# Layer 2 of a four-layer graph network: scores transposed, one constant shift in the softmax, row sums by a column of ones

## The chip, the cores and the metric

The kernel runs on one core of one Trainium2 chip. The metric is the device time of one execution in microseconds. The kernel before takes 2988.76 us, the median of three runs (2983.72, 2988.76 and 2989.16).

The engines are called by their names in the profile: PE is TensorE (matrix products and transposes; PEld are its weight loads), DVE is VectorE, ACT is ScalarE, POOL is GpSimd, SP is SyncE, whose queue issues most loads and stores.

## The reference, cut to what matters

The input x has 32 graphs of 512 nodes with 256 features, in float32. One adjacency matrix of 512 by 512 integers holds for all graphs; about 1 entry in 16 is set, and the diagonal is. Four layers follow each other, and after each one stands `x = layernorm(x + layer(x))`:

- Layer 0: attention with 8 heads under the mask, then a two-matrix network with two layer norms of its own.
- Layer 1: attention whose scores are sums of two numbers, one for each node, through a leaky ReLU.
- Layer 2, the one that changes: full scores between all nodes.
- Layer 3: like layer 1 with 4 heads, and an ELU at its end.

Layer 2 computes, for each graph:

```python
h1, h2, h3 = x @ W1, x @ W2, x @ W3          # 512 x 256 each
e = leaky_relu(h1 @ h2.T, 0.2)               # 512 x 512
e = where(adj > 0, e, -1e12)
out = relu(softmax(e, axis=-1) @ h3)
```

A softmax doesn't change when the same number is subtracted from every score of a row. Any number that keeps the exponentials in the range of float32 will do; the row's maximum always does.

## The kernel before, in words

**Tiles.** A graph's x lies in SBUF as 4 blocks (`NC`) of 128 nodes on the partitions, with 256 features (`KC` = 2 blocks of 128). `transposed` (L857 to L871) turns it on PE into a buffer with the features on the partitions. A matrix product on PE takes two operands with the contracted index on the partitions: one of 128 columns is loaded as weights, the other, of up to 512 columns, streams through; the result lands in one of 8 PSUM banks of 512 columns. Each float32 product is two records in the profile, so the counts of matmuls are twice those of the calls; transposes are one record each.

**Layer 2** (`layer2`, L1186 to L1243). W1 and W2 are multiplied once, in `prepare`, into `l2m`, with the sign turned (L847, `scale=-1.0`). So the kernel before works on the negative scores:

- L1190: q = x·l2m, transposed; L1191: v = x·W3.
- For each block c of 128 query nodes: L1200 makes their negative scores against all 512 keys in one bank. ACT scales them by 0.2 into `lo` (L1203), DVE takes the minimum of both (L1206), which is the negative leaky ReLU. L1208, one fused DVE operation, adds the mask and brings each row's minimum along in an accumulator. ACT takes the exponential with that minimum as bias, and sums each row in its own accumulator (L1213). DVE inverts the sum (L1216).
- The exponentials have the queries on the partitions, and the last product needs the keys there. So L1223 transposes them, 16 blocks of 128x128, and ACT copies four banks to `pT` (helper line L854, shown as p<-bank).
- L1234 multiplies by v, two query blocks in one bank; ACT takes the ReLU with the inverted sum as scale (L1239), and POOL adds x (`add`, L924).

Layer 1 (L1158 to L1184) already has the other form: its exponentials have the keys on the partitions, v carries a column of ones (L1161, a POOL memset), L1175 multiplies with 257 columns so that column 257 is the row sum, and DVE inverts it out of the bank (L1180).

**The order of the work.** Every instruction is first entered in a plan: engine, a duration in ns, what it reads and writes, and for transfers a lag until they land. The planner (`place`, L507 to L609) simulates the engines with these durations and emits each engine's instructions in one fixed order. Up to `WAYS` = 5 graphs are in flight. A graph may begin when the one 5 places before it has ended in the plan. Among instructions that could start at the same time, the one with the earliest due time goes first; due times come from `PACE`, `TENTHS`, `START` and `LAST` (numbers in us at the head of the file). PE has different tilings (full array, 32-row, 32- or 64-column parts); `STAY` is what the planner holds against changing the tiling.

**Buffers.** `KINDS` (L659 to L665) gives the number of buffers of each kind: 5 for x (`x`), 8 of 128x2048 (`p`), 18 small ones (`rs`), and so on, plus 8 banks. A graph's result is stored out of its x buffer at L1326, with a lag of 3000 ns in the plan.

**Ranges.** The fast path is followed by a check: some layers use forms that only hold in a range, and `fit`, `far` and `odd` collect whether all values were inside. If not, `general_path` runs after it.

Of the kernel before, what the change touches and what calls it, by code (L numbers as in the profile page):

```python
# [9 lines left out]
FP = mybir.dt.float32  # L10
BF = mybir.dt.bfloat16
I32 = mybir.dt.int32
# [10 lines left out]
R_MIN, R_MAX = 1e-30, 1e20  # L23
H0, H3 = 8, 4
# [3 lines left out]
PACE = 90.76  # L28
START = (0, 17.91, 74.63, 79.1, 135.8)
LAST = ()  # L30
STAY = 3.96
TENTHS = (0, 30.43, 93, 94.94, 170.51, 206.64, 280.32, 312.71, 390.11, 382.2, 480.41)
# [411 lines left out]
class Plan:  # L444
# [62 lines left out]
    def place(self, urgency, ways, stay=0.0, run=True):  # L507
# [35 lines left out]
        while todo:  # L543
# [58 lines left out]
            ended[op.graph] = max(ended.get(op.graph, 0.0), done)  # L602
# [9 lines left out]
def fast_path(  # L612
# [47 lines left out]
        "x": (5, [P, NC, C]), "y": (7, [P, NC, C]), "v": (3, [P, NC, C + 2 * H3]),  # L660
# [15 lines left out]
    nc.gpsimd.memset(eps, EPS)  # L676
    ones = const.tile([P, P], FP, name="ones")
# [47 lines left out]
    odd = keep("odd", [P, NC])  # L725

    def prepare():
# [34 lines left out]
        for m in range(NC):  # L762
            bank = Slot("bank")

            def run(bank=bank, m=m):
# [5 lines left out]
                [bank], [(edge_t, m)])  # L771

# [20 lines left out]
        for c in range(NC):  # L793
            off = Slot("e")
            dve(690, lambda c=c: nc.vector.tensor_scalar(
                T(mask)[:, c, :], T(raws[c // 2])[:, c % 2, :].bitcast(I32), 0.0, BIG, ALU.is_le, ALU.mult),
                [(raws[c // 2], c)], [(mask, c)])
# [39 lines left out]
        for k in range(KC):  # L837
            bank = Slot("bank")

            def run(bank=bank, k=k):  # L840
# [6 lines left out]
                T(l2m)[:, k, :], T(bank)[:, :C], AF.Copy, scale=-1.0), [bank], [(l2m, k)])  # L847
        load(l2w3, lambda t: t, rows(l2_w3))
        scored(l3w, l3_w, l3_a, H3)
# [153 lines left out]

    def skip(n):

        for _ in range(n):
            plan(DMA, 0, None)

    def layer0(xs, at_once):
# [58 lines left out]
        def check():  # L1068
            r = T(rinv)[:, :NC * H0]
            nc.vector.scalar_tensor_tensor(fit, r, R_MIN, fit, ALU.is_gt, ALU.min)  # L1070
            nc.vector.scalar_tensor_tensor(fit, r, R_MAX, fit, ALU.is_lt, ALU.min)
        dve(370, check, [rinv], [], True)
# [113 lines left out]
    def layer2(xs):  # L1186
        xT = transposed(xs)
        qT, v, p, pT, y = Slot("t"), Slot("v"), Slot("p"), Slot("p"), Slot("y")
        for k in range(KC):
            project_t(l2m, k * P, xT, qT, k)  # L1190
        project(xT, l2w3, 0, C, v)  # L1191
        rinvs = []
        for c in range(NC):
            bank, lo, es = Slot("bank"), Slot("e"), Slot("e")
            low, tot, rinv = Slot("rs"), Slot("rs"), Slot("rs")
            rinvs.append(rinv)

            def run(bank=bank, c=c):
                for k in range(KC):
                    nc.tensor.matmul(T(bank), T(qT)[:, k, c * P:(c + 1) * P], T(xT)[:, k, :],  # L1200
                                     start=(k == 0), stop=(k == KC - 1))
# [3 lines left out]

            dve(690, lambda bank=bank, lo=lo, es=es: nc.vector.tensor_tensor(  # L1206
                T(es), T(bank), T(lo), ALU.min), [bank, lo], [es])
            dve(780, lambda es=es, low=low, c=c: nc.vector.tensor_tensor_reduce(  # L1208
                T(es), T(es), T(mask)[:, c, :], 1.0, TOP, ALU.add, ALU.min, T(low)[:, 0:1]),
                [es, (mask, c)], [es, low], True)  # L1210

            def exp(es=es, low=low, tot=tot, rinv=rinv, c=c):
                nc.scalar.activation(T(p)[:, c, :], T(es), AF.Exp, bias=T(low)[:, 0:1],  # L1213
                                     scale=-1.0, accum_out=T(tot)[:, 0:1])
            act(935, exp, [es, low], [(p, c), tot])
            dve(160, lambda tot=tot, rinv=rinv: nc.vector.reciprocal(  # L1216
                T(rinv)[:, 0:1], T(tot)[:, 0:1]), [tot], [rinv])
        for m in range(NC):
            bank = Slot("bank")

            def run(bank=bank, m=m):
                for c in range(NC):
                    nc.tensor.transpose(T(bank)[:, c * P:(c + 1) * P],  # L1223
                                        T(p)[:, c, m * P:(m + 1) * P], ident)
# [182 lines left out]
```

## Time and profile before

| | before |
|---|---|
| device time, median of 3 | 2988.76 us |
| span of the profiled execution | 2983.3 us |
| PE busy | 2901.5 us, 97% |
| PE weight loads busy (beside PE) | 1645.9 us, 55% |
| DVE busy | 2371.4 us, 79% |
| ACT busy | 1962.9 us, 66% |
| POOL busy | 946.7 us, 32% |
| mean granted TensorE clock | 0.990 |

A row of the groups reads: line, engine, operation, output<-inputs, shapes, count | busy us, mean ns of one | idle time of the engine just before, and what ended it. Matmuls overlap on PE, so the mean length of one is longer than the time it holds the engine; the distance from one start to the next tells that. In a waits line stand engine and what it was about to do, what it waited for, the sum in us, how often, and the longest. The span is the time from the first to the last instruction on the chip.

### The profile page before, as it was taken

To read this page: it belongs to the slowest core of one execution; us is meant where nothing else is said; L and a number is where in the kernel's file an instruction comes from. 1 tells how busy PE (TensorE), PEld (TensorE's weight loads), DVE (VectorE), ACT (ScalarE), POOL (GpSimd) and SP (SyncE) were. 2 spreads that over 40 slices of the span, in tenths; PEclk is the share of its full clock that TensorE was granted. 3 is DMA by queue.
4 is the path that set the end of the run, shared out by engine and by line. 5 is a ranking of instruction groups with operands and counts; after the bars stand their busy time and mean duration, and the time that the engine had idled before them with its cause. 6 is when DMAs were issued, how large, how long until landed. Compare 5 with 4: busy or idle time off the path is not lost.

```text
span 2983.3 us, 41104 instructions
## 1 busy us (share of the span) xinstructions
PE 2901.5 (97%) x14770; PEld 1645.9 (55%) x14770; DVE 2371.4 (79%) x4138; ACT 1962.9 (66%) x4359; POOL 946.7 (32%) x865
## 2 busy tenths in 40 slices
PE   7899999999999999999999999999999999999895
PEld 3455555555555555555555555555555555555552
DVE  5567788888887888888888888887888888877785
ACT  4656776666776666776666776666776666776562
POOL 0222343322333322333322333322333322333211
PEclk9999999999999999999999999999999999999998
DMA  6545665566565566666566565566665566563232
GB/s 170 115 89 108 145 133 118 128 147 139 126 138 115 128 147 139 130 135 122 127 148 139 127 141 117 127 147 133 131 138 117 127 147 140 128 138 80 52 89 72
DMA packets 93714, 375.75 MB, mean 126 GB/s; under 512 B 8768, under 2 KB 44736, under 8 KB 57664
## 3 DMA queue, kind: packets, MB, share of 16 engines
q0 software_dynamic: 44640, 292.57, 50.0%
q1 hardware_dynamic: 48864, 80.49, 8.0%
q8 instruction: 118, 1.93, 0.3%
q14 instruction: 92, 0.75, 0.1%
HBM read 63.38 MB, written 17.10 MB: 27 GB/s over the span
## 4 chain that ended last, share of the span: by engine, by line
PE 93%; DVE 3%; DMA 2%; ACT 1%; issue 0%; POOL 0%; SPq 0%; ACTq 0%; DVEq 0%
PE bank L893 15%; PE bank L879 11%; PE bank L996 9%; PE bank L1049 8%; PE bank L1175 8%; PE bank L1234 7%; PE bank L1278 7%; PE bank L1200 7%; PE bank L866 5%; PE bank L1102 4%; PE bank L1090 4%; PE bank L1021 2%; PE bank L1223 2%; PE bank L979 2%; PE bank L1253 1%; PE bank L947 1%
## 5 line engine op out<-in xcount | busy, mean ns | idle before, releaser
L934 POOL DMA_DIRECT2D p<-p x310 | 280.7, 908 | 1228.5 <-issue 290.2
L1042 DVE TENSOR_TENSOR p<-p,edge_t 128x2048 f32<-128x2048 f32 x256 | 602.5, 2355 | 78.9 <-ACT p L1000 78.6
L1000 ACT ACTIVATE p<-bank 128x512 f32<-128x512 f32 x1024 | 559.7, 597 | 137.7 <-PE bank L996 137.5
L854 ACT ACTIVATE t<-bank 128x512 f32<-128x512 f32 x640 | 372.4, 594 | 367.2 <-PE bank L879 147.3
L924 POOL TENSOR_TENSOR y<-y,x 128x512 f32<-128x512 f32 x192 | 339.0, 1769 | 377.6 <-ACT y L1239 173.9
L907 DVE BATCH_NORM_STATS2 st<-y 128x6 f32<-128x256 f32 x768 | 315.3, 411 | 67.7 <-POOL y L924 60.1
L1269 DVE TENSOR_TENSOR p<-p,edge_t 128x2048 f32<-128x2048 f32 x128 | 292.9, 2288 | 3.3
L996 PE MATMUL bank<-t,t 32*128 32x512 f32 x2048 | 294.4, 643 | 0.0
L917 ACT ACTIVATE x<-y,rs,rs 128x256 f32<-128x256 f32 x512 | 283.4, 595 | 7.2 <-DVE rs L914 6.5
L1262 DVE TENSOR_SCALAR p<-p,e,e 128x512 f32<-128x512 f32 x512 | 252.0, 545 | 36.6 <-DMA p<-row 32.6
L1049 PE MATMUL bank<-p,v 128*32 128x512 f32 x2048 | 269.3, 607 | 11.8 <-DVE p L1042 11.7
L1175 PE MATMUL bank<-v,p 128*128 128x257 f32 x1024 | 249.5, 389 | 11.8 <-DVE p L1168 11.8
L1278 PE MATMUL bank<-p,v 128*64 128x512 f32 x1024 | 236.5, 603 | 12.6 <-DVE p L1269 12.6
L854 ACT ACTIVATE v<-bank 128x258 f32<-128x258 f32 (+2 forms) x384 | 171.8, 455 | 111.7 <-PE bank L893 108.5
L1200 PE MATMUL bank<-t,t 128*128 128x512 f32 x512 | 238.7, 599 | 0.0
L879 PE MATMUL bank<-t,wqkv 128*128 128x512 f32 x512 | 233.0, 606 | 3.2 <-ACT t L854 3.2
L1175 PEld LDWEIGHTS bank<-v,p 128*128 128x128 f32 x1024 | 190.8, 193 | 73.9 <-issue 29.7
L1234 PE MATMUL bank<-v,p 128*128 128x256 f32 x1024 | 230.2, 382 | 0.0
L1234 PEld LDWEIGHTS bank<-v,p 128*128 128x128 f32 x1024 | 191.6, 190 | 49.1 <-ACT t L854 20.5
L917 ACT ACTIVATE y<-y,rs,rs 128x256 f32<-128x256 f32 x256 | 138.9, 595 | 62.9 <-DVE rs L914 62.9
L996 PEld LDWEIGHTS bank<-t,t 32*128 32x128 f32 x2048 | 81.1, 183 | 166.6 <-issue 76.5
L866 PEld LDWEIGHTS bank<-ident,x 128*128 128x128 f32 x1024 | 117.4, 142 | 99.4 <-issue 61.3
(116 smaller groups left out, 4487.1 us busy)
## 6 DMA issues: line engine op xcount, KB each, us to landing
p<-p POOLq DMA_DIRECT2D x248, 1024.0 KB, 7.6
p<-row SPq DMA_DIRECT2D x32, 1024.0 KB, 8.9
p<-p POOLq DMA_DIRECT2D x62, 512.0 KB, 5.7
x<-in_x_dram SPq DMA_DIRECT2D x32, 512.0 KB, 3.9
out_dram<-x SPq DMA_DIRECT2D x32, 512.0 KB, 2.9
e<-row SPq DMA_DIRECT2D x32, 256.0 KB, 6.7
t<-in_adj_dram SPq DMA_DIRECT2D x4, 256.0 KB, 6.3
wqkv<-in_L_gnn_w_qkv_dram SPq DMA_DIRECT2D x1, 768.0 KB
```

Of the source, the lines that this page charges most:

```text
L854: act(170 + n * 0.84, lambda: nc.scalar.activation(to(T(dst)), frm(T(src)), AF.Copy), [src], writes)
L879: nc.tensor.matmul(T(bank), T(w)[:, i, col:col + P], T(xT)[:, i, :], start=(i == 0), stop=(i == KC - 1))
L893: nc.tensor.matmul(T(bank)[:, j * width:(j + 1) * width], T(xT)[:, k, (c0 + j) * P:(c0 + j + 1) * P], T(w)[:, k, col:col + width], start=( ...
L917: act(600, lambda c=c: nc.scalar.activation(T(dst)[:, c, :], T(y)[:, c, :], AF.Identity, bias=T(nm)[:, c:c + 1], scale=T(rs)[:, c:c + 1]), ...
L996: nc.tensor.matmul(T(banks[j]), T(kT)[r, g, m * P:(m + 1) * P], T(qT)[r, g, :], start=True, stop=True)
L1000: act(600, lambda j=j: nc.scalar.activation(T(p)[:, j, :], T(banks[j]), AF.Exp, scale=1.0 / math.sqrt(D0)), [banks[j]], [(p, j)])
L1042: dve(2420, lambda p=p, m=m: nc.vector.tensor_tensor(T(p), T(p), T(edge_t)[:, m, :].unsqueeze(1).to_broadcast([P, J, N]), ALU.mult), [p, ( ...
L1049: nc.tensor.matmul(T(av)[j * D0:(j + 1) * D0, :], T(v)[:, m, h * D0:(h + 1) * D0], T(p)[:, j, :], start=(m == 0), stop=(m == NC - 1))
L1175: nc.tensor.matmul(T(bank)[:, :C + 1], T(p)[:, m, c * P:(c + 1) * P], T(v)[:, m, 2:C + 3], start=(m == 0), stop=(m == NC - 1))
L1200: nc.tensor.matmul(T(bank), T(qT)[:, k, c * P:(c + 1) * P], T(xT)[:, k, :], start=(k == 0), stop=(k == KC - 1))
L1234: nc.tensor.matmul(T(bank)[:, j * C:(j + 1) * C], T(pT)[:, m, c * P:(c + 1) * P], T(v)[:, m, :C], start=(m == 0), stop=(m == NC - 1))
L1278: nc.tensor.matmul(T(av)[i * D3:(i + 1) * D3, :], T(q)[:, m0 + m, 2 * H3 + h * D3:2 * H3 + (h + 1) * D3], T(p)[:, 2 * m + i, :], start=(m0 ...
```

## The change

The scores of layer 2 are computed with the keys on the partitions (the two operands of the product swap places). Then the exponentials come out in the layout that the last product needs as weights, and the 16 transposes and four copies of each graph go. A maximum along a row can't be taken there, since a row now lies across partitions. So one constant, 72, is subtracted from all scores, and the row sums come from a column of ones beside v, as in layer 1. The constant only works within limits: the inverted row sums are compared with `R2_MIN` and `R2_MAX`, and the columns of W3 with a bound; outside of them the general path runs. The mask is made from the transposed adjacency, with the other sign.

Four further edits concern the plan: a sixth buffer for x, a lag of 8000 ns instead of 3000 for the store, a graph's end in the plan that no longer includes the lag of its last transfer, and new numbers at the head of the file.

```diff
@@ -21,15 +21,18 @@
 TOP = 3e38
 S_MAX = 40.0
 R_MIN, R_MAX = 1e-30, 1e20
+SHIFT = 72.0
+R2_MIN, R2_MAX = 1.25e-37, 1e31
+V_MAX = 41.0
 H0, H3 = 8, 4
 
 
 WAYS = 5
-PACE = 90.76
-START = (0, 17.91, 74.63, 79.1, 135.8)
-LAST = ()
-STAY = 3.96
-TENTHS = (0, 30.43, 93, 94.94, 170.51, 206.64, 280.32, 312.71, 390.11, 382.2, 480.41)
+PACE = 90.30
+START = (0, 22.9, 53.29, 85.04, 134.37)
+LAST = (-0.21, 0.21)
+STAY = 4.86
+TENTHS = (0, 26.21, 86.69, 92.24, 176.51, 212.02, 277.3, 313.49, 381.31, 382.21, 490.27)
 @with_exitstack
 def general_path(
     ctx: ExitStack,
@@ -599,7 +602,7 @@
             left.remove(op.rank)
             while front[op.graph] not in left and left:
                 front[op.graph] += 1
-            ended[op.graph] = max(ended.get(op.graph, 0.0), done)
+            ended[op.graph] = max(ended.get(op.graph, 0.0), t + op.ns + SIGNAL)
             if not left:
                 del todo[op.graph]
                 order.remove(op.graph)
@@ -657,7 +660,7 @@
 
 
     KINDS = {
-        "x": (5, [P, NC, C]), "y": (7, [P, NC, C]), "v": (3, [P, NC, C + 2 * H3]),
+        "x": (6, [P, NC, C]), "y": (7, [P, NC, C]), "v": (3, [P, NC, C + 2 * H3]),
         "t": (9, [P, KC, N]), "p": (8, [P, 4, N]), "e": (4, [P, N]),
         "st": (6, [P, NC, 6]), "mv": (6, [P, NC, 2]), "rs": (18, [P, NC]),
         "e1": (6, [P, NC * H3]), "gs": (2, [P, NC * H3]), "ri": (3, [P, NC * H0]),
@@ -674,6 +677,8 @@
     make_identity(nc, ident)
     eps = const.tile([P, 1], FP, name="eps")
     nc.gpsimd.memset(eps, EPS)
+    shift = const.tile([P, 1], FP, name="shift")
+    nc.gpsimd.memset(shift, -SHIFT)
     ones = const.tile([P, P], FP, name="ones")
     nc.gpsimd.memset(ones, 1.0)
 
@@ -722,7 +727,7 @@
 
 
     edge_t, mask = keep("edge_t", [P, NC, N], BF), keep("mask", [P, NC, N], BF)
-    odd = keep("odd", [P, NC])
+    odd = keep("odd", [P, NC + 1])
 
     def prepare():
         def load(dst, to, src, lag=15000):
@@ -769,6 +774,9 @@
             plan(PE, 440, run, [edges], [bank])
             dve(690, lambda bank=bank, m=m: nc.vector.tensor_copy(T(edge_t)[:, m, :], T(bank)),
                 [bank], [(edge_t, m)])
+            dve(400, lambda m=m: nc.vector.tensor_scalar(
+                T(mask)[:, m, :], T(edge_t)[:, m, :], 1.0, BIG, ALU.subtract, ALU.mult),
+                [(edge_t, m)], [(mask, m)])
 
 
 
@@ -792,9 +800,6 @@
 
         for c in range(NC):
             off = Slot("e")
-            dve(690, lambda c=c: nc.vector.tensor_scalar(
-                T(mask)[:, c, :], T(raws[c // 2])[:, c % 2, :].bitcast(I32), 0.0, BIG, ALU.is_le, ALU.mult),
-                [(raws[c // 2], c)], [(mask, c)])
             dve(690, lambda c=c, off=off: nc.vector.tensor_tensor(
                 T(off), T(edges)[:, c, :], T(raws[c // 2])[:, c % 2, :].bitcast(I32), ALU.not_equal),
                 [edges, (raws[c // 2], c)], [off])
@@ -844,8 +849,23 @@
                                      start=(d == 0), stop=(d == KC - 1))
             plan(PE, 870, run, wt, [bank])
             act(400, lambda bank=bank, k=k: nc.scalar.activation(
-                T(l2m)[:, k, :], T(bank)[:, :C], AF.Copy, scale=-1.0), [bank], [(l2m, k)])
+                T(l2m)[:, k, :], T(bank)[:, :C], AF.Copy), [bank], [(l2m, k)])
+
+
         load(l2w3, lambda t: t, rows(l2_w3))
+        sq, bank, wide = Slot("e"), Slot("bank"), Slot("e")
+        act(600, lambda: nc.scalar.activation(T(sq), flat(T(l2w3)), AF.Square), [l2w3], [sq])
+
+        def run():
+            for k in range(KC):
+                nc.tensor.matmul(T(bank)[:, :C], ones, T(sq)[:, k * C:(k + 1) * C],
+                                 start=(k == 0), stop=(k == KC - 1))
+        plan(PE, 870, run, [sq], [bank])
+        dve(400, lambda: nc.vector.tensor_scalar(
+            T(wide)[:, :C], T(bank)[:, :C], V_MAX ** 2 / C, None, ALU.is_gt), [bank], [wide])
+        dve(400, lambda: nc.vector.tensor_reduce(
+            T(odd)[:, NC:NC + 1], T(wide)[:, :C], mybir.AxisListType.X, ALU.max),
+            [wide], [(odd, NC)])
         scored(l3w, l3_w, l3_a, H3)
 
 
@@ -1001,6 +1021,12 @@
                 T(p)[:, j, :], T(banks[j]), AF.Exp, scale=1.0 / math.sqrt(D0)),
                 [banks[j]], [(p, j)])
 
+    def within(r, low, high):
+
+        seen = fit[:, :r.shape[-1]]
+        nc.vector.scalar_tensor_tensor(seen, r, low, seen, ALU.is_gt, ALU.min)
+        nc.vector.scalar_tensor_tensor(seen, r, high, seen, ALU.is_lt, ALU.min)
+
     def skip(n):
 
         for _ in range(n):
@@ -1065,11 +1091,7 @@
         rinv = rinv0(sm)
         t = heads_out(oT, rinv, H0)
 
-        def check():
-            r = T(rinv)[:, :NC * H0]
-            nc.vector.scalar_tensor_tensor(fit, r, R_MIN, fit, ALU.is_gt, ALU.min)
-            nc.vector.scalar_tensor_tensor(fit, r, R_MAX, fit, ALU.is_lt, ALU.min)
-        dve(370, check, [rinv], [], True)
+        dve(370, lambda: within(T(rinv)[:, :NC * H0], R_MIN, R_MAX), [rinv], [], True)
         for c0 in range(0, NC, 2):
             add(t, t, xs, c0)
         n1 = Slot("y")
@@ -1185,61 +1207,43 @@
 
     def layer2(xs):
         xT = transposed(xs)
-        qT, v, p, pT, y = Slot("t"), Slot("v"), Slot("p"), Slot("p"), Slot("y")
+        qT, v, p, y, rinv = Slot("t"), Slot("v"), Slot("p"), Slot("y"), Slot("rs")
         for k in range(KC):
             project_t(l2m, k * P, xT, qT, k)
+        plan(POOL, 110, lambda: nc.gpsimd.memset(T(v)[:, :, C:C + 1], 1.0), [xT], [(v, "one")])
         project(xT, l2w3, 0, C, v)
-        rinvs = []
-        for c in range(NC):
+        for m in range(NC):
             bank, lo, es = Slot("bank"), Slot("e"), Slot("e")
-            low, tot, rinv = Slot("rs"), Slot("rs"), Slot("rs")
-            rinvs.append(rinv)
-
-            def run(bank=bank, c=c):
+
+            def run(bank=bank, m=m):
                 for k in range(KC):
-                    nc.tensor.matmul(T(bank), T(qT)[:, k, c * P:(c + 1) * P], T(xT)[:, k, :],
+                    nc.tensor.matmul(T(bank), T(xT)[:, k, m * P:(m + 1) * P], T(qT)[:, k, :],
                                      start=(k == 0), stop=(k == KC - 1))
             plan(PE, 1720, run, [qT, xT], [bank])
             act(600, lambda bank=bank, lo=lo: nc.scalar.activation(
                 T(lo), T(bank), AF.Copy, scale=0.2), [bank], [lo])
-
             dve(690, lambda bank=bank, lo=lo, es=es: nc.vector.tensor_tensor(
-                T(es), T(bank), T(lo), ALU.min), [bank, lo], [es])
-            dve(780, lambda es=es, low=low, c=c: nc.vector.tensor_tensor_reduce(
-                T(es), T(es), T(mask)[:, c, :], 1.0, TOP, ALU.add, ALU.min, T(low)[:, 0:1]),
-                [es, (mask, c)], [es, low], True)
-
-            def exp(es=es, low=low, tot=tot, rinv=rinv, c=c):
-                nc.scalar.activation(T(p)[:, c, :], T(es), AF.Exp, bias=T(low)[:, 0:1],
-                                     scale=-1.0, accum_out=T(tot)[:, 0:1])
-            act(935, exp, [es, low], [(p, c), tot])
-            dve(160, lambda tot=tot, rinv=rinv: nc.vector.reciprocal(
-                T(rinv)[:, 0:1], T(tot)[:, 0:1]), [tot], [rinv])
-        for m in range(NC):
+                T(es), T(bank), T(lo), ALU.max), [bank, lo], [es])
+            dve(690, lambda es=es, m=m: nc.vector.tensor_tensor(
+                T(es), T(es), T(mask)[:, m, :], ALU.add), [es, (mask, m)], [es], True)
+            act(600, lambda es=es, m=m: nc.scalar.activation(
+                T(p)[:, m, :], T(es), AF.Exp, bias=shift), [es], [(p, m)])
+        for c in range(NC):
             bank = Slot("bank")
 
-            def run(bank=bank, m=m):
-                for c in range(NC):
-                    nc.tensor.transpose(T(bank)[:, c * P:(c + 1) * P],
-                                        T(p)[:, c, m * P:(m + 1) * P], ident)
-            plan(PE, 440, run, [p], [bank])
-            evac(pT, lambda t, m=m: t[:, m, :], bank, lambda b: b, N, [(pT, m)])
-        for c0 in range(0, NC, 2):
-            bank = Slot("bank")
-
-            def run(bank=bank, c0=c0):
-                for j in range(2):
-                    c = c0 + j
-                    for m in range(NC):
-                        nc.tensor.matmul(T(bank)[:, j * C:(j + 1) * C],
-                                         T(pT)[:, m, c * P:(c + 1) * P], T(v)[:, m, :C],
-                                         start=(m == 0), stop=(m == NC - 1))
-            plan(PE, 3470, run, [pT, v], [bank])
-            for j in range(2):
-                act(470, lambda bank=bank, j=j, c=c0 + j: nc.scalar.activation(
-                    T(y)[:, c, :], T(bank)[:, j * C:(j + 1) * C], AF.Relu,
-                    scale=T(rinvs[c])[:, 0:1]), [bank, rinvs[c0 + j]], [(y, c0 + j)])
-            add(y, y, xs, c0)
+            def run(bank=bank, c=c):
+                for m in range(NC):
+                    nc.tensor.matmul(T(bank)[:, :C + 1], T(p)[:, m, c * P:(c + 1) * P],
+                                     T(v)[:, m, :C + 1], start=(m == 0), stop=(m == NC - 1))
+            plan(PE, 1740, run, [p, v], [bank])
+            dve(160, lambda bank=bank, c=c: nc.vector.reciprocal(
+                T(rinv)[:, c:c + 1], T(bank)[:, C:C + 1]), [bank], [(rinv, c)])
+            act(470, lambda bank=bank, c=c: nc.scalar.activation(
+                T(y)[:, c, :], T(bank)[:, :C], AF.Relu, scale=T(rinv)[:, c:c + 1]),
+                [bank, (rinv, c)], [(y, c)])
+            if c % 2:
+                add(y, y, xs, c - 1)
+        dve(250, lambda: within(T(rinv), R2_MIN, R2_MAX), [(rinv, c) for c in range(NC)], [], True)
         return y
 
     def layer3(xs, at_once):
@@ -1324,7 +1328,7 @@
             xs = Slot("x")
             normalise(y, xs)
         plan(SP, 450, lambda: nc.sync.dma_start(
-            out[b].rearrange("(c p) d -> p c d", p=P), T(xs)), [xs], [], lag=3000)
+            out[b].rearrange("(c p) d -> p c d", p=P), T(xs)), [xs], [], lag=8000)
```

## The prediction

> **What bounds the kernel now.** I read the busy shares first, then the busy time by stretch, then the waits of TensorE, and last the rows of layer 2. The page of the kernel before says who is full:
>
> ```profile
> PE 2901.5 (97%) x14770; PEld 1645.9 (55%) x14770; DVE 2371.4 (79%) x4138; ACT 1962.9 (66%) x4359; POOL 946.7 (32%) x865
> PE   7899999999999999999999999999999999999895
> ```
>
> 97% is a mean. The table by stretch (length, then busy us and instructions of PE, PEld, DVE, ACT, POOL, then clock) shows where the other 3% lie:
>
> ```profile
> 0.00:75.00 75.00, 59.30 (x296) 26.66 (x296) 40.30 (x78) 37.50 (x73) 7.31 (x18) 0.93 0.69 171
> 1000.00:2000.00 1000.00, 999.96 (x5141) 571.31 (x5134) 826.54 (x1418) 681.03 (x1513) 338.49 (x304) 1.00 0.62 133
> 2850.00:2925.00 75.00, 64.98 (x298) 42.08 (x297) 58.53 (x117) 38.46 (x93) 17.82 (x17) 0.99 0.37 85
> 2925.00:2984.00 59.00, 28.23 (x122) 13.38 (x122) 30.35 (x54) 16.03 (x36) 7.07 (x8) 0.76 0.26 69
> ```
>
> In the middle TensorE is never idle, VectorE is at 83% and ScalarE at 68%. Of the 82 us that PE idles in the whole span, 23 fall before 150 us (the same table) and 49 after 2700: filling and draining. So in the middle the time is the sum of TensorE's instructions, and each one taken off it counts in full; what is taken off DVE or ACT counts only where it lets PE go on. The waits (engine and line, what it waited for, sum, times, longest) agree:
>
> ```profile
> PE bank L866 <- DMA x<-in_x_dram: 12.4, 3, 7.9
> PE bank L1175 <- DVE p L1168: 11.8, 3, 7.3
> DVE rs L1180 <- PE bank L1175: 81.3, 63, 2.8
> POOL y L924 <- ACT y L1239: 173.9, 58, 12.3
> ```
>
> PE's two longest sums are small. Between 150 and 2700 us PE waited 4.5 us, in 2 waits, for a graph's input (L866); the other 7.9 is the start. DVE waits far longer for PE (81.3 us at L1180) than PE for DVE.
>
> The rows of layer 2 that the change touches (busy us, mean ns | idle before):
>
> ```profile
> L1223 PE MATMUL bank<-ident,p 128*128 128x128 f32 x512 | 72.0, 276 | 1.8 <-ACT p L1213 1.8
> L854 ACT ACTIVATE p<-bank 128x512 f32<-128x512 f32 x128 | 71.9, 599 | 77.9 <-PE bank L1223 77.9
> L1234 PE MATMUL bank<-v,p 128*128 128x256 f32 x1024 | 230.2, 382 | 0.0
> L1208 DVE CUSTOM_DVE_ANT_0 e<-e,mask 128x512 f32<-128x512 f32 x128 | 88.6, 692 | 4.2
> L1213 ACT ACTIVATE p<-e,rs 128x512 f32<-128x512 f32 x128 | 91.2, 713 | 5.9 <-DVE rs L1208 5.5
> L1213 ACT ACTIVATION_READ_ACCUMULATOR p<-e,rs 128x1 f32 x128 | 24.3, 190 | 0.0
> L1208 DVE DVE_READ_ACCUMULATOR2_ANT rs<- 128x1 f32 x128 | 10.5, 82 | 0.0
> ```
>
> A matmul's 276 ns is not its price: they overlap. Its price is the distance from one start to the next in the timeline of PE (start, length, line, count):
>
> ```profile
> 1002.01 0.60 PE L1223 MATMUL bank<-ident,p 128*128 128x128 f32 x4
> 1002.45 1.89 PE L893 MATMUL bank<-wqkv,t 128*128 128x256 f32 x8
> ...
> 1011.96 7.17 PE L1234 MATMUL bank<-v,p 128*128 128x256 f32 x32
> 1019.06 1.14 PE L996 MATMUL bank<-t,t 32*128 32x512 f32 x8
> ...
> 1030.59 1.90 PE L1175 MATMUL bank<-v,p 128*128 128x257 f32 x8
> 1032.33 1.04 PE L979 MATMUL bank<-ident,t 128*128 128x128 f32 x8
> ```
>
> Four transposes hold PE for 1002.45 − 1002.01 = 0.44 us, 110 ns each. Eight records of 257 columns (layer 1) hold it for 1.74 us, 217 ns each; 32 of 256 columns for 7.10, 222 each with a change of tiling at the end.
>
> [...] after a gap from 116.2 to 119.4 us the seven 128x512 matmuls of L879 take 6.13 us, some 850 ns each instead of 430, so such a gap costs its length and about 3 us more. [...] the rows show 682 (L1206) and 692 (the fused L1208), so the plain mask addition should cost what the fused one did. [...]
>
> **The change part by part.** Scores are computed with keys on the partitions, so the exponentials come out as the stationary operand that the last product needs.
>
> 1. PE, removed: 16 transposes a graph, 512 in all. At 110 ns that is 56.3 us. Over the middle stretch the start-to-start time of L1223 is 53.5 us for 453 records, 118 each, since some carry a stall or a change of tiling: 60.5 for 512. Part of the surplus belongs to the neighbours and will stay; I take 58.
>
> 2. PE, added: one column of ones in each product. 217 against 216 ns a record (the commonest start-to-start times of L1175 and L1234), times 1024: 1 us. The product now goes out as four pieces of 1.74 us, not two of 3.47, so 64 more boundaries can fall on a change of tiling; one costs 0.09 us (309 against 217 ns). Between 0 and 6 us; I take 1, because neighbouring pieces usually stay together. The score matmuls only swap their operands at the same shape: 0. In preparation two 128x256 products, 0.9 us. PE net: 58 − 3 = 55 us.
>
> 3. ACT: 128 evacuations of 599 ns (71.9) and 128 accumulator reads (24.3) go, and the exponential falls from 713 towards the 597 of L1000 (14.8): 111 us, from 68% to about 65% in the middle. Worth nothing directly, because PE's own work hides it.
>
> 4. DVE: the accumulator reads go (10.5). A range check comes: two operations of at most 192 and 223 ns (L1070, L1071 on wider data) a graph, at most 13 us. Minimum becomes maximum, and the fused add a plain one: 0. DVE stays near 2372 us, which at a shorter span is 81%, or 85% in the middle. POOL gets 32 memsets of 462 ns (L1161): 15 us, beside 2000 idle.
>
> 5. A new wait: the reciprocal now reads the bank after the product. It stands in DVE's order as layer 1's does, which waited 81.3 us over 128 (L1180). Behind it are the multiplications that feed PE in the other graphs (L1042, L1262); after it come relu, addition and normalisation of the same graph. It replaces the 26.7 us that L1216 waited for ACT. Extra DVE idle: 0 to 55 us in total. PE has five graphs in flight and was waiting for DVE some 25 us in all, nearly all in the ends, so I count 0 on PE and keep up to 27 for the range (half of it coming through).
>
> 6. The sixth input buffer, and a graph's end counted without its store: the input's load no longer needs the buffer of the graph just stored. This takes the two waits of 4.5 us in the middle; the load itself lands in 3.9 us beside 100% PE. Worth 0 to 4.5; I take 4. The store's lag of 8 us instead of 3 only orders the plan, since the store on the chip lands in 2.9 us.
>
> 7. Filling and draining: layer 2 of one graph alone loses its transposes and the last evacuation, from 2905.2 to 2908.3 us in the last one, some 3 us of latency. But the whole order is laid out anew with other start times and due times, and the ends hold 72 us of idle PE plus half-clocked stretches. Sign unknown, ±15; I take 0.
>
> Sum: 2988.8 − 55 − 4 = 2929.8, and I say **2930**, 2.0% less.
>
> **The rivals.** (A) The forecast: PE stays full, its work shrinks. 2930. (B) Also the ends shrink: shorter chains in layer 2, more free p buffers (one for layer 2 instead of two, of eight) and earlier loads. If a quarter of the 82 us of idle goes: 2910. For it: the drain is a chain of single waits; against it: most of that drain is layer 1 and layer 3 on DVE (L1262, L1269), untouched. (C) PE gets holes, because DVE at 85% with reciprocals that wait for PE delays the masks: half of the 55 us of point 5 gives 2930 + 27 = 2957. For it: the 81.3 us at L1180; against it: PE is at 999.96 of 1000 with those already there. (D) Slower: the new order leaves one hole a graph. A hole of 2.2 us in each of 32 graphs makes 70 us, 3000; [...] For it: nothing in the middle; only the fact that every start is moved. The range check of the shift could also send the program to the general path after the fast one, which would cost far more; the reference's inputs give logs of the shifted row sums from −66.7 to 83.7, worked out in double precision, between the limits of −71.4 and 85.0, so I leave this out.
>
> **How the numbers follow.** A 0.60, B 0.15, C 0.17, D 0.08. Faster by over 0.2% (below 2982.8): A, B and nearly all of C, 0.91; within 0.2%: 0.02; slower: 0.07. The range takes in B's centre and most of C: 2906 to 2955. Its lower end is A with point 1 at its most, 60.5, no loss in point 2 and 15 us less in the ends; the upper end is A with 25 us more of holes or of drain.
>
> **What would show it.** L1223 and the evacuation p<-bank gone; PE busy near 2846; PE over 99.5% busy from 1000 to 2000 us, with more graphs done in it; the product with 257 columns at 217 ns from start to start; the new reciprocal waiting for PE by 50 to 110 us; no wait for a graph's input after the first. The prediction is wrong if PE shows idle in the middle (C, D), if the product's pieces cost more than 1.8 us each, or if the stretches before 150 us and after the last full one together differ from 72 us of idle by over 15.

## The result, and the profile after

The changed kernel takes **2972.11 us** (median of 4 runs, 2967.91 to 2973.78) against 2988.96 for the kernel before beside it: a ratio of 0.9943, with a 95% interval of 0.9925 to 0.9961. It is faster, by 17 us and not by the 59 forecast, and outside of the range of 2906 to 2955.

The page of the changed kernel, as shown for the one before:

```profile
PE 2866.9 (97%) x14262; PEld 1585.3 (53%) x14262; DVE 2293.7 (77%) x4076; ACT 1889.8 (64%) x4104; POOL 958.9 (32%) x898
PE   8899999999999999999999999999999999999885
```

PE is still 97% busy, but its busy time fell by 35 us only, and its idle time rose from 82 to 102. The table by stretch (columns as before):

```profile
0.00:75.00 75.00, 62.04 (x316) 28.70 (x316) 41.64 (x80) 39.35 (x77) 7.33 (x19) 0.98 0.74 177
1000.00:2000.00 1000.00, 992.57 (x4977) 549.95 (x4976) 794.45 (x1413) 658.47 (x1433) 351.54 (x318) 0.99 0.62 133
2850.00:2925.00 75.00, 60.83 (x234) 37.38 (x234) 38.97 (x80) 33.65 (x72) 11.50 (x15) 0.86 0.32 74
2925.00:2970.00 45.00, 17.38 (x78) 5.09 (x78) 27.34 (x51) 9.13 (x19) 3.81 (x4) 0.70 0.12 43
```

The middle has a hole that it didn't have: 992.57 of 1000 us, and a clock of 0.99. The waits of PE name it:

```profile
PE bank L1075 <- DVE p L1068: 27.0, 13, 4.2
PE bank L1197 <- DVE rs L934: 14.8, 2, 11.0
PE bank L886 <- ACT x L937: 12.8, 4, 4.8
PE bank L1257 <- DVE p L1273: 12.0, 1, 12.0
PE bank L886 <- DMA x<-in_x_dram: 7.6, 1, 7.6
```

The two waits for an input in the middle are gone (only the first, 7.6 us, is left). In their place PE waits 27 us for L1068, the mask of layer 0 on DVE, 20.1 of them between 150 and 2700 us. Before the change that mask is L1042, and PE never waited for it in the middle; this sum lies in the ends:

```profile
PE bank L1049 <- DVE p L1042: 11.7, 6, 2.8
```

The other waits of the changed kernel shown above lie in filling and draining.

The rows of the new layer 2:

```profile
L1236 PE MATMUL bank<-v,p 128*128 128x257 f32 x1024 | 243.6, 386 | 0.0
L1229 ACT ACTIVATE p<-e,shift 128x512 f32<-128x512 f32 x128 | 91.7, 717 | 2.0 <-DVE e L1227 2.0
L1227 DVE TENSOR_TENSOR e<-e,mask 128x512 f32<-128x512 f32 x128 | 88.3, 690 | 3.3
L1239 DVE RECIPROCAL rs<-bank 128x1 f32<-128x1 f32 x128 | 20.7, 163 | 100.8 <-ACT p L1020 63.8 <-PE bank L1236 36.9
L1241 ACT ACTIVATE y<-bank,rs 128x256 f32<-128x256 f32 x128 | 61.2, 480 | 169.8 <-DVE rs L1239 169.7
```

Transposes and evacuations are gone. The plain mask addition costs 690 ns (the fused one 692). The new reciprocal has DVE idle for 100.8 us before it (the profile puts 36.9 down to the product and 63.8 to an exponential on ACT), and the ReLU behind it has ACT idle for 169.7, new as well. Whether that costs time is one of the questions below.

**PE's time taken apart.** I add up, for all matmuls of a run, the distance from one start to the next, and split it by the usual price of each shape and what goes beyond it (us; the last but one column is the prediction's term):

| | before | after | forecast | measured |
|---|---|---|---|---|
| transposes at their usual price (109 ns) | 289.1 | 233.1 | −58 | −56.0 |
| products at their usual price | 2419.2 | 2422.7 | +2 | +3.5 |
| changes of tiling, other stalls below 0.15 us each | 168.9 | 175.6 | +1 | +6.7 |
| holes and half-clocked matmuls, 150 to 2700 us | 14.5 | 37.3 | −4 | **+22.8** |
| the same before 150 and after 2700 us | 69.3 | 76.0 | 0 | +6.7 |
| sum | 2961.1 | 2944.8 | −59 | −16.3 |

So the work fell as forecast, and the greater part of the loss is holes in the middle.

**Where a hole comes from.** A hole is a stretch in which PE starts nothing. Five are alike, of 2.8 to 4.4 us, after 515, 697, 878, 1058 and 1766 us, each after the products of L913 and ahead of L1075. (A sixth, of 4.6 us, after 296 us, has another cause and stays in all runs of this order; it is taken up at the end.) The chain of waits around the fourth (start, length, what):

```profile
1040.86 3.39 DMA row<-gT
...
1044.39 10.21 DMA p<-row
...
1054.73 1.00 DVE p L1266 x2
...
1057.21 0.04 DVE p L1273
1057.25 2.17 issue
1059.42 2.29 DVE p L1068
1061.71 0.04 issue
1061.76 1.29 PE bank L1075 x8
```

And PE in the same stretch:

```profile
1054.50 3.72 PE L913 MATMUL bank<-l2w,t 128*128 128x256 f32 x16
1061.76 1.29 PE L1075 MATMUL bank<-p,v 128*32 128x512 f32 x8 [3.54 <-DVE p L1068]
1062.98 3.36 PE L1282 MATMUL bank<-p,v 128*64 128x512 f32 x8
```

DVE just before:

```profile
1054.73 1.00 DVE L1266 TENSOR_SCALAR p<-p,e,e 128x512 f32<-128x512 f32 x2 [5.26 <-DMA p<-row]
```

Layer 3 brings its gates, one row for all partitions, by a transfer (p<-row, L1168 in the changed kernel). L1266 on DVE multiplies by them. Here the transfer landed 10.2 us after its issue; DVE stood idle for 5.26 us ahead of L1266, and behind that in DVE's fixed order stood L1068, the mask of another graph, for which PE waited. After the hole eight records of L1282 take 3.36 us; 24 of them took 5.37 at 1003.70, so 1.8 for eight. The granted clock was 0.50 from 1062.5 to 1065.8 us, against 1.00 from 1003 to 1009. Behind each of the five holes it is 0.50, for 3.4 us behind the first four and for 6.8 behind the fifth. So the hole costs its length and a stretch at half clock.

Why was it late? GpSimd's queue around the same time, and the queue of SP:

```profile
1043.04 0.88 POOL L954 DMA_DIRECT2D p<-p  x1 [2.58 <-DMA p<-p]
```
```profile
1044.39 0.33 SPq L1168 DMA_DIRECT2D p<-row  x1
```

An accumulating transfer p<-p, 1 MB, was issued 1.35 us ahead of the gates. One graph later, where PE has no hole, it came 0.22 us after them:

```profile
1135.53 0.90 POOL L954 DMA_DIRECT2D p<-p  x1 [3.61 <-DMA p<-p]
```
```profile
1135.31 0.33 SPq L1168 DMA_DIRECT2D p<-row  x1
```

The time from issue to the first sign of landing is 3.8 to 5.8 us in 28 of the 32 graphs and 9.0 to 9.3 in four, issued at 502.4, 683.5, 864.2 and 1044.4: ahead of four of the five holes. (In the fifth the accumulation was issued 0.3 us ahead. Of the gates' 128 DMA records of 8 KB all but five start within 5.5 us of the issue; the last five follow each other by 0.93 us, and DVE waited until 11.7 us after the issue.)

This gives **theory H**: the work fell as forecast; the new order of the instructions places L1266, and behind it a mask that PE needs, where a late gate transfer stops DVE, and the transfer is late where an accumulation gets ahead of it. **Rival R**: the reciprocal that waits for the product holds DVE up. **Rival P**: the four plan edits spoil the order, the rewrite alone would do better. Two more names stand in the expectations below. Theory N: an order is good only with planner numbers that were fitted to its operations. Theory X: the new order needs the sixth input buffer together with the earlier end of a graph.

### The profile page after: what moved, and what is told of

Read it like the earlier page. It is cut to its first block, busy times and chain, and to the rows that moved or that the text cites. A ratio compares the mean times of both kernels' runs of the same rounds, so it can differ in the third digit from the quotient of the medians.

```text
span 2969.2 us, 39737 instructions
## 1 busy us (share of the span) xinstructions
PE 2866.9 (97%) x14262; PEld 1585.3 (53%) x14262; DVE 2293.7 (77%) x4076; ACT 1889.8 (64%) x4104; POOL 958.9 (32%) x898
## 4 chain that ended last, share of the span: by engine, by line
PE 90%; DVE 4%; DMA 3%; ACT 1%; issue 1%; POOL 0%; SPq 0%; ACTq 0%; DVEq 0%
PE bank L913 15%; PE bank L899 10%; PE bank L1016 8%; PE bank L1075 8%; PE bank L1197 8%; PE bank L1236 8%; PE bank L1282 8%; PE bank L1220 8%; PE bank L886 5%; PE bank L1112 4%; PE bank L1124 3%; PE bank L1047 2%; DMA p<-row 2%; PE bank L999 2%; PE bank L1257 1%; PE bank L967 1%
## 5 line engine op out<-in xcount | busy, mean ns | idle before, releaser
L954 POOL DMA_DIRECT2D p<-p x310 | 273.9, 886 | 1520.4 <-DMA p<-p 522.2
L1020 ACT ACTIVATE p<-bank 128x512 f32<-128x512 f32 x1024 | 546.9, 604 | 156.3 <-PE bank L1016 156.1
L1068 DVE TENSOR_TENSOR p<-p,edge_t 128x2048 f32<-128x2048 f32 x256 | 592.9, 2319 | 56.3 <-ACT p L1020 55.0
L1075 PE MATMUL bank<-p,v 128*32 128x512 f32 x2048 | 276.8, 614 | 27.8 <-DVE p L1068 27.0
L1273 DVE TENSOR_TENSOR p<-p,edge_t 128x2048 f32<-128x2048 f32 x128 | 293.1, 2290 | 3.2
L1266 DVE TENSOR_SCALAR p<-p,e,e 128x512 f32<-128x512 f32 x512 | 252.9, 539 | 31.6 <-DMA p<-row 31.1
L937 ACT ACTIVATE x<-y,rs,rs 128x256 f32<-128x256 f32 x512 | 269.5, 597 | 9.2 <-DVE rs L934 9.2
L1197 PE MATMUL bank<-v,p 128*128 128x257 f32 x1024 | 249.2, 390 | 19.6 <-DVE rs L934 14.8
L1236 PE MATMUL bank<-v,p 128*128 128x257 f32 x1024 | 243.6, 386 | 0.0
L1282 PE MATMUL bank<-p,v 128*64 128x512 f32 x1024 | 242.7, 614 | 0.4 <-DVE p L1273 0.4
L1197 PEld LDWEIGHTS bank<-v,p 128*128 128x128 f32 x1024 | 192.4, 194 | 59.1 <-issue 34.4
L1241 ACT ACTIVATE y<-bank,rs 128x256 f32<-128x256 f32 x128 | 61.2, 480 | 169.8 <-DVE rs L1239 169.7
L886 PEld LDWEIGHTS bank<-ident,x 128*128 128x128 f32 x1024 | 119.1, 144 | 88.5 <-ACT x L937 36.6
```

Source lines behind the costliest of these rows:

```text
L1020: act(600, lambda j=j: nc.scalar.activation(T(p)[:, j, :], T(banks[j]), AF.Exp, scale=1.0 / math.sqrt(D0)), [banks[j]], [(p, j)])
L1068: dve(2420, lambda p=p, m=m: nc.vector.tensor_tensor(T(p), T(p), T(edge_t)[:, m, :].unsqueeze(1).to_broadcast([P, J, N]), ALU.mult), [p, ( ...
L1075: nc.tensor.matmul(T(av)[j * D0:(j + 1) * D0, :], T(v)[:, m, h * D0:(h + 1) * D0], T(p)[:, j, :], start=(m == 0), stop=(m == NC - 1))
L1197: nc.tensor.matmul(T(bank)[:, :C + 1], T(p)[:, m, c * P:(c + 1) * P], T(v)[:, m, 2:C + 3], start=(m == 0), stop=(m == NC - 1))
L1236: nc.tensor.matmul(T(bank)[:, :C + 1], T(p)[:, m, c * P:(c + 1) * P], T(v)[:, m, :C + 1], start=(m == 0), stop=(m == NC - 1))
L1282: nc.tensor.matmul(T(av)[i * D3:(i + 1) * D3, :], T(q)[:, m0 + m, 2 * H3 + h * D3:2 * H3 + (h + 1) * D3], T(p)[:, 2 * m + i, :], start=(m0 ...
```

## The experiments

All times are medians; the kernel before had 2988 to 2989 us beside them. Where an edit leaves the plan alone, the instructions stay in the changed kernel's order, and the run tells what that instruction or transfer costs in this order. Where an edit changes the plan, all is laid out anew.

**The gate transfer cut to a quarter**, same order:

```diff
-to = lambda: flat(T(G))
+to = lambda: flat(T(G))[:, :N]
-to(), T(row)[:R, :].rearrange("r q -> (r q)").partition_broadcast(P)),
+to(), T(row)[:NC, :].rearrange("r q -> (r q)").partition_broadcast(P)),
```

> The changed kernel in exactly its own order, but layer 3's gate transfer brings the rows of one head in place of four (256 KB in place of 1 MB); the other heads read what the buffer held. Left out: three quarters of that transfer, so layer 3's output is another one. Theory H: the five holes of about 4 us at PE's masked product of layer 0, each followed by a half-clocked stretch, go; 20 to 27 us less than the changed kernel, some 2947, and the waits of VectorE for the row go from 31 us to below 8. Rivals P and R: the holes stay, within 5 us of 2972.

Measured: 2949.8 us, ratio 0.9874 (0.9858 to 0.9891), 22 us below the changed kernel. DVE's waits for the row fall from 31.1 us to 12.1, not below 8: in five graphs the cut transfer is still behind an accumulation and shows its landing after 6.5 to 6.8 us, but the longest wait is now 2.9 us in place of 5.9. The middle is full again:

```profile
1000.00:2000.00 1000.00, 1000.00 (x5053) 557.44 (x5052) 802.45 (x1426) 674.39 (x1469) 357.16 (x321) 1.00 0.60 125
```

and PE's waits for L1068 are 11.6 us in place of 27.0:

```profile
PE bank L1075 <- DVE p L1068: 11.6, 11, 2.7
```

**The reciprocal without its wait**, same order:

```diff
-nc.vector.reciprocal(T(rinv)[:, c:c + 1], T(bank)[:, C:C + 1])
+nc.vector.tensor_scalar(T(rinv)[:, c:c + 1], T(v)[:, c, C:C + 1], 1e-30, None, ALU.mult)
```

> The changed kernel in its own order, but VectorE's reciprocal of the row sum, which waits for the product in the bank, becomes a multiplication of v's column of ones by 1e-30, which waits for nothing late. Left out: the normalisation of layer 2 (its output is nearly nothing beside x). Theory H: the holes in the middle stay, within 6 us of 2972. Rival R: they go, 20 us or more below, about 2950, and with them the waits of VectorE for products of the other graphs.

Measured: 2969.7 us, ratio 0.9938 (0.9922 to 0.9955): 2.4 us below the changed kernel, within its spread. The holes stay:

```profile
PE bank L1075 <- DVE p L1068: 22.2, 12, 4.3
```

DVE's idle time only moved: its waits of L1068 for the exponentials (L1020) rose from 55.0 to 107.6 us. Rival R falls.

**The accumulations cut to half**, same order:

```diff
-a, b = (T(dst), T(src)) if src else (T(dst)[:, 0:2, :], T(dst)[:, 2:4, :])
+a, b = (T(dst)[:, 0:2, :], T(src)[:, 0:2, :]) if src else (T(dst)[:, 0:2, :], T(dst)[:, 2:4, :])
```

> The changed kernel in its own order, but each accumulating transfer p<-p of a whole buffer adds half of its columns (512 KB in place of 1 MB). Left out: half of the row sums of layers 0 and 3. If the gate transfer is late because it lies behind an accumulation (theory H): the latest gate lands some 3 us sooner, the holes at PE's masked product of layer 0 shrink by as much, and the time falls to 2945 to 2960. If the gate is late by itself: the holes stay at 3 to 4.6 us, 2968 to 2975.

Measured: 2945.0 us, ratio 0.9855 (0.9839 to 0.9872), 27 us below the changed kernel, with the gate transfer at its full size. Its first sign of landing comes 3.8 to 6.3 us after the issue in all 32 graphs, and PE's waits for L1068 are down to:

```profile
PE bank L1075 <- DVE p L1068: 8.6, 7, 2.7
```

Holes and half clock in the middle take 10.3 us, less than the 14.5 before the change. So the gates are late because of the accumulations. The DMA records say how: in the late case, from 0 to 4 us after the gates' issue, GpSimd's queue moves 96 records and SP's none; in the other order SP's queue moves 104 in these 4 us and GpSimd's none. The first record of the gates starts 4.1 to 5.0 us after the issue in the four late graphs, and after 0.9 to 1.2 in all others. The trace has 128 records of 8 KB for such a transfer. In the fourth hole the accumulation goes nearly through first: 112 of its records start ahead of the gates' first, and the other 16 ahead of the gates' seventeenth. In the fifth hole the last five records of the gates start 0.93 us apart, which is about one record of the gates (0.32 us) and one of the accumulation (0.63). What decides which queue moves next was not shown by any run here.

**The gates in four transfers, and in two**, same order, all of the work (the code is cut to layer 3's case):

```diff
-nc.sync.dma_start(to(), T(row)[:R, :].rearrange("r q -> (r q)").partition_broadcast(P))
+[nc.sync.dma_start(T(G)[:, h, :],
+   T(row)[h * NC:(h + 1) * NC, :].rearrange("r q -> (r q)").partition_broadcast(P))
+ for h in range(heads)]              # two transfers: heads h and h + 1, in steps of 2
```

> The changed kernel in its own order with all of its work, but layer 3's gate transfer is issued as four of 256 KB, one for each head, so that the first masked head waits for its own quarter alone. Theory H: the first quarter lands some 2 to 4 us sooner, the holes at PE's masked product of layer 0 go or shrink to below 1.5 us: 2947 to 2960. If a transfer that is queued behind an accumulation moves nothing until that one is done, the first quarter is as late as the whole was: within 4 us of 2972.

> The changed kernel in its own order with all of its work, the gate transfer as two pieces of two heads. VectorE needs heads 0 and 1 first. If the first piece lands in time more often than a whole gate, as with four pieces: 2955 to 2966. If only the quarter is short enough: within 4 us of 2972.

Measured: 2961.9 us with four (0.9907, 0.9891 to 0.9924) and 2963.0 with two (0.9911, 0.9894 to 0.9927). Both do all of the work and are faster than the kernel before and, in their medians, than the changed one, by 10 and 9 us. They get less than half of what the cut transfers get, and four pieces miss theory H's 2947 to 2960 by a little. With four pieces PE still waits:

```profile
PE bank L1075 <- DVE p L1068: 23.7, 15, 3.0
```

The first quarter shows its landing after 2.1 to 2.9 us where it is ahead of an accumulation, and after 6.7 to 7.4 where it is behind; here the smaller pieces didn't get past an accumulation issued before them. The longest hole is 3.0 us, not below 1.5. DVE's waits for the gates rise in sum to 37.0 us, in 16 waits, but none is longer than 4.4 us.

**The same on the kernel before**, in its own order:

> The kernel before in its own order, with layer 3's gate transfer as four of 256 KB. Theory H: its order has TensorE waiting for no mask behind a late gate, so nothing is to be had: within 6 us of 2989. If the late gate had cost there as well: 15 us or more below.

Measured: 2989.5 us, ratio 1.0005 (0.9998 to 1.0012). In the kernel before, the gates landed later than after the change (first sign at 8.2 us in the median, against 5.5), and DVE waited as long for them (32.6 us against 31.1). An accumulation was issued 1.0 to 2.9 us ahead of them in 22 graphs there, and in 4 after the change. With the split DVE's waits for the gates fall to 3.2 us, and the time stays: they cost nothing there. Two things differ between the orders, and no run takes them apart. The waits before are many and short, 22 of at most 2.5 us, and after the change 9 of up to 5.9; and behind them stood no mask that PE waited for in the middle, as L1068 does after the change.

**The transposes put back** as dead work, in the changed kernel's order (the edit, written out as two loops):

```diff
-for m in range(NC):
-    nc.tensor.matmul(T(bank)[:, :C + 1], T(p)[:, m, c * P:(c + 1) * P], ...)
+for m in range(NC):
+    nc.tensor.transpose(T(bank)[:, m * P:(m + 1) * P], T(p)[:, m, c * P:(c + 1) * P], ident)
+for m in range(NC):
+    nc.tensor.matmul(T(bank)[:, :C + 1], T(p)[:, m, c * P:(c + 1) * P], ...)
```

> The changed kernel in its own order, with 16 transposes a graph put back on TensorE as dead work: four into the bank of each product piece, which the product then overwrites. If TensorE's own work is the time (theory H): 512 times 110 ns, 56 us more than the changed kernel, 3028, or a little less, 3015 to 3028, where the added work falls into the holes. If TensorE has slack that hid the saving: less than 20 us more.

Measured: 3017.1 us, ratio 1.0105 (1.0084 to 1.0125), 45 us above the changed kernel. By the same sum as in the table, transposes rise by 55.9 us, while holes and half clock fall from 113 to 100 us and the small stalls by 2: part of the work fills holes. So PE's work is the time: at the price that the prediction took in the sum, and four fifths of it, 45 us, in this run.

**The rewrite alone, the plan edits alone, and the rewrite with the old numbers**, each in a new order:

```
 l2_alone:   the new layer 2; x buffers 5, store lag=3000, graph's end with lag, old PACE/START/LAST/STAY/TENTHS
 plan_alone: the old layer 2; x buffers 6, store lag=8000, graph's end without lag, new PACE/START/LAST/STAY/TENTHS
 l2_oldnums: the new layer 2 and plan edits; old PACE/START/LAST/STAY/TENTHS
```

> Layer 2 rewritten alone: five input buffers, store lag of 3000 ns, a graph's end with its last lag, and the numbers at the head of the file as before the change. TensorE's work falls by some 53 us here as well. Theory H (the loss sits where VectorE waits at the head of its queue for layer 3's gate transfer, and depends on where an order happens to put that wait): a time anywhere between 2935 and 2975, with fewer or other holes in the middle than the full change. Rival P (the four plan edits spoil the order): near 2940, clearly below 2972. Rival R (the reciprocal behind the product is to blame, in any order): 2968 or more, with as much PE idle in the middle.

> The four plan edits and the new head numbers alone, on the old layer 2 with its transposes. Theory H: no change of TensorE's work, so within 15 us of 2989, the sign left open. Rival P (the edits cost what is missing): 20 us or more above 2989. If the edits were what gains: below 2975.

> The rewritten layer 2 with the sixth buffer, the store's lag of 8000 ns and the graph's end without its lag, but with the five numbers at the head of the file as before the change. If the numbers have to fit the operations (theory N): well above the kernel before, 3050 to 3200, like the rewrite alone. If it was the buffer and the lags that the rewrite alone lacked: 2960 to 2990.

Measured: 3149.0, 3593.1 and 3258.0 us. Theory H said 2935 to 2975 and about 2989 for the first two and missed both by far: the rewrite alone is 161 us slower than the kernel before. Rival P falls for the rewrite alone as well, which it had near 2940. The second is above 2989, as rival P has it, but on the old layer 2, to which the new numbers were not fitted. The third lies above even the 3050 to 3200 of theory N. All three agree with theory N, which no run tests by fitting numbers anew. PE's work is what it should be (transposes 233 us in the first and third, 289 in the second); the rest is holes and slowed matmuls, and of another sort each time. In the second PE waits in nearly every graph for an accumulation:

```profile
PE bank L1253 <- DMA p<-p: 247.6, 29, 9.4
```

**One plan edit undone, in a new order each**: five x buffers, or the lag of the store in a graph's end.

```diff
 x5:     -"x": (6, [P, NC, C])          +"x": (5, [P, NC, C])
 endlag: -max(..., t + op.ns + SIGNAL)  +max(..., done)
```

> The changed kernel with five input buffers in place of six, all else as changed; the planner lays out another order. If the sixth buffer is what the new order needs (theory X): PE waits for inputs or has holes in most graphs, 3000 or more. If it only removes the two waits for an input that the kernel before showed: 2972 to 2980.

> The changed kernel with a graph's end in the plan counted with the lag of its store again (8 us now), all else as changed. If the sixth buffer is only of use together with the earlier end (theory X): like the run with five buffers, 3000 or more. If the end is a detail: 2965 to 2985.

Measured: 3070.0 and 3064.7 us. Both are above 3000, as theory X has it, and within 6 us of each other. But what PE waits for isn't the input (8.4 and 8.6 us, once each, at the start), it is the mask of layer 0, with a hole at the same place in nearly every graph. With five buffers:

```profile
PE bank L1075 <- DVE p L1068: 62.3, 58, 2.7
PE bank L886 <- ACT x L937: 21.2, 29, 4.8
```

The traces show the chain of theory H once more, now in most graphs: an accumulation was issued 0.9 to 3 us ahead of the gates in 25 of them, DVE waits 112.0 us for the gates with five buffers and 111.5 with the lag, in 27 waits each (31.1 us in 9 in the changed kernel), and each of PE's 24 holes between L913 and L1075 follows such a wait. What the buffer is worth by itself the runs don't give.

**The planner told that the gates land later**, in new orders:

```diff
-plan(DMA, 750 * heads, None, [row, started], [G], lag=2500)
+plan(DMA, 750 * heads, None, [row, started], [G], lag=2500 if heads == 1 else 5000)   # and 7000
```

> The changed kernel, with the planner told that the gate transfer of layer 3 lands 2.5 us later (a lag of 5000 ns in place of 2500); it lays out another order. If knowing the landing is what the order lacked: VectorE's waits for the row go and the time falls to 2945 to 2960. If an order is good only with numbers fitted to just its durations (theory N): above 2990.

> The same with a lag of 7000 ns, which covers the latest landing seen (about 10 us after the issue). As for the lag of 5000: 2945 to 2960 if knowing the landing suffices; above 2990 if theory N holds.

Measured: 3626.3 and 3697.9 us. A landing planned 2.5 or 4.5 us later, meant for the late transfers, made the order worse by more than 650 us. DVE's waits for the gates fall to 9.8 us with the lag of 5000, but again PE waits for an accumulation in nearly every graph (with the lag of 7000: 227.5 us in 30 waits). With 5000:

```profile
PE bank L1257 <- DMA p<-p: 254.3, 31, 9.4
PE bank L1075 <- DVE p L1068: 90.6, 32, 3.2
```

In all, the seven orders laid out from settings that weren't fitted to their operations took 3065 to 3698 us, as theory N has it.

## Why the prediction was wrong

**Right**: that PE's work is the time, and its price. Transposes removed: 58 forecast, 56.0 in the sum, 45 net when put back. The product with a column of ones, the mask addition, the vanished waits for inputs, and the reciprocal's waits without much effect on PE (2.4 us, within the spread): as forecast. The forecast had it wait 50 to 110 us for PE; it waits 36.9 for PE and 100.8 in all.

**Point 7 failed**, "the whole order is laid out anew … Sign unknown, ±15; I take 0", and with it the sentence of A that PE stays full. I read the 999.96 us of 1000 as a property of the work, with DVE at 83% as a reserve. It is a property of one order. The new order had 22.8 us more of holes and half clock in the middle, and 22 and 27 us go when the gates or the accumulations are cut. So the step that failed is the 0 for the new order, and the ±15 around it was too narrow. How far orders differ is shown only roughly: seven others lay 76 to 710 us above the kernel before, with settings that weren't fitted.

**Rival C** had the right size for the middle (27 us of holes through DVE) by luck, since the cause was another. I looked for what the change adds to DVE's order, the reciprocal; freed, it gave 2.4 us. The wait that cost was an old one, for p<-row, of nearly the same total before and after (32.6 and 31.1 us). I had it before me in the row of L1262, idle 36.6 us, of which 32.6 for p<-row, and left it out because it cost nothing there. Here is that row of the kernel before, and DVE's wait after the change:

```profile
L1262 DVE TENSOR_SCALAR p<-p,e,e 128x512 f32<-128x512 f32 x512 | 252.0, 545 | 36.6 <-DMA p<-row 32.6 <-DMA p<-p 2.3 <-PE bank L879 0.9
```
```profile
DVE p L1266 <- DMA p<-row: 31.1, 9, 5.9
```

**Point 5** asked who stands behind the waiting reciprocal, but no point asked it of the waits that were there already.

**Point 2** was above its upper end, if all 6.7 us of changes of tiling and small stalls are its own, where I took 1. In the trace, between 150 and 2700 us, 114 records of the product stand 93 to 104 ns longer than the rest, against 56 before; 58 of them are followed by another tiling, against 27 before. That the cut into four pieces is the cause was not tried alone.

**Points 3 and 4** were off in size, without consequence: ACT fell by 73 us and not by 111, among other things because the exponential from SBUF with a bias still takes 717 ns and not the 597 that I took from one out of PSUM. DVE fell by 78 us where I had none. Two slips change nothing: the lower end of the range, added up from its parts, is 2909 and not 2906, and the longest sum of waits of PE was 12.6 us (L1278 for L1269), all in the ends, and not the 12.4 that I showed first.

Of the 42 us between forecast and result, 27 are so in the middle (22.8 more, where I had 4 less), 6 in tilings and stalls, 7 in the ends and 3 in the prices of transposes and products; the forecast's 59 against 16 by the sum of the table makes 43. Open is why the ends grew: their waits (L1197 for L934, 11.0 us, L1257 for L1273, 12.0) stand in all runs of this order, and none was taken away.

## What to carry to other kernels

A saving on a full engine counts in full only in an order that keeps it full; where a planner lays the order out anew, the order is part of the change, and its spread can't be read from the idle time of the one at hand. For each wait in an engine's fixed order ask how long it is at a time and what stands behind it, for old waits too: some 32 us for the gates cost nothing in one order, in short pieces, and 22 in the other. And to see what an order loses to one transfer or one instruction, shorten that alone with the order held; here a plan that expected the transfer later brought something worse.

## What the runs showed of the hardware that was not expected

- A transfer of SP's queue issued 1.35 us behind an accumulation of GpSimd showed its landing after 9.2 us, and the median of the 32 is 5.5; cut to a quarter or behind accumulations of half size it was no longer late enough to stop PE for long.
- A hole of 3.5 us on PE was followed by matmuls at half their speed (3.36 us for eight, against 1.8, at a granted clock of 0.50), so the five holes, 19 us in sum, cost more than their length: 22 us go when the gates are cut.
- The same DVE multiplication of layer 1, 128x512, took 1318 ns in the mean before and 650 after, with shape, type and count as they were:

```profile
L1165 DVE TENSOR_SCALAR p<-e,e,e 128x512 f32<-128x512 f32 x128 | 165.5, 1318 | 1.0 <-PE bank L1021 1.0
```
```profile
L1187 DVE TENSOR_SCALAR p<-e,e,e 128x512 f32<-128x512 f32 x128 | 75.7, 650 | 0.1
```

Beside an addition of GpSimd's lay 60 of the 128 before, which took 2185 ns in the mean, and 35 after, with 940; the others took 553 and 541. That the additions are the cause was not shown: no run here takes them away. The 89.8 us are more than the whole fall of DVE's busy time. On PE the stretched multiplications stand behind one hole of each kernel: before, 3.4 us after 153 us, and after the change the sixth hole of the middle, where four multiplications, one of them of 4.59 us beside three additions, hold up the mask of layer 1 (L1190):

```profile
292.45 5.96 DVE L1187 TENSOR_SCALAR p<-e,e,e 128x512 f32<-128x512 f32 x4
```
```profile
PE bank L1197 <- DVE p L1190: 4.8, 2, 4.6
```
